# Half-size transposes on both row halves, a new order of a step, and padded last rows in a local-attention branch

## The chip, the cores and the metric

The kernel runs on one core of a Trainium2 chip. A core has a TensorE (PE, with its weight loads shown apart as PEld), a VectorE (DVE), a ScalarE (ACT), a GpSimd (POOL) and queues that issue DMAs (SyncE, SP, here). Each engine works through its own instructions in the order in which they were issued and waits on semaphores for the others. PE writes its results to PSUM, of which there are eight banks of 128 partitions by 512 fp32 values, and DVE or ACT carry them from there to SBUF. The metric is the time of one execution in microseconds (us) as the device takes it.

## The reference

The input `x` has 2 sequences of 2048 tokens with 256 features, all in fp32. It is normalized first (`xn`), and then

- the first branch `s` is a global attention with 16 heads of 16 features and a spatial bias on the first 257 rows and columns, a projection, and a layer norm of `xn` added to it;
- the second branch is two layers of a local transformer on `xn`, and `g` is the SiLU of what it returns;
- the output is `x + s * g`.

A layer of the second branch is, for every sequence:

```
h   = shift_token(x)                     # second half of the features comes from the token before
q,k,v = split(h @ wqkv)                  # 8 heads of 64
q,k = l2norm(q)*q_scale, l2norm(k)*k_scale, then rotary with the xpos scale
o   = softmax(mask(8 q k^T)) v           # windows of 128, each sees itself and the window before
x   = x + o @ wo
h   = layernorm(shift_token(x))*lg + lb
a,g = split(h @ w1 + b1)                 # 2 x 682
x   = x + (a * gelu(g)) @ w2 + b2
```

682 is five blocks of 128 and 42 rows more.

## The kernel before

`global_attention` computes the first branch and puts it into DRAM (`s_out`). It takes the first 1790 us and is not touched. `ffn_branch` computes the second branch and the output.

**Tiling.** The residual stream lies transposed in SBUF, features on partitions, as `xA[b]`, one tile for each sequence. The branch walks through 16 chunks (`slots`): layer, chunk of 512 tokens, sequence, in that order from the outermost. A chunk (`s`) has four tiles of 128 tokens (`i`), which are also the attention's windows. The loop at the end of the function takes one step for every tile, `n = 4 s + i`, and four more to drain. In a step several tiles are in work at once: `cur` is the tile of the step, `pre` the one before it and `pre2` the one before that.

**The pieces of a step.** The order of the instructions on each engine is the order in which the code issues them (the scheduler is off: `tc.manual_schedule()`). The string `STEP` gives the order of the pieces, and `FIRST_STEP` that of the first nine steps:

- `Q`, `K`, `V` (`a_project`, L844): the projection of `cur`, two products of 512 columns each. DVE multiplies Q and K out of PSUM by the rotary tables (L861 to L863), ACT squares them (L865) and POOL adds the two halves of the rotation (L866). `norm`, issued after the next piece but one, sums the squares (L870), takes a maximum with a tiny number (L874) on DVE, the power -1/2 (L875) and the product (L876) on POOL. V is copied by ACT (L850).
- `T0`, `T1` (`a_turn`, L888): four transposes of `pre`'s rotated Q and K by PE into one bank, and one copy to SBUF, of Q by ACT (L891) and of K by DVE (L894).
- `S0`, `S1` (`a_scores`, L913): the scores of `pre`, for four of the eight heads each. A head has 64 features, so that two heads, on rows 0 to 63 and 64 to 127 of the array, go into two banks. DVE adds the mask and takes the maximum (L926), ACT exponentiates with a running sum (L934), DVE inverts the sums (L940) and POOL multiplies by them (L948); in the first eight tiles ACT does this (L945).
- `W0`, `W1` (`a_weights`, L961): the transposes of the attention weights, eight of 128x128 for four heads, and their copies, by DVE for the first four heads (L968) and by ACT for the others (L966).
- `A0`, `A1` (`a_sums`, L982): weights times V, with the output on 64 partitions, and after `A1` a copy by ACT (L990).
- `F`: what else is due in this step for older chunks: the variance product `pv` (`f_var`, L1034) at `i = 0`, the attention's output projection `px` (`a_out`, L997) at `i = 1`, half of the second feed-forward product (`f_out`) at `i = 2` and at `i = 3`, the sum over the halves (`f_add`) at `i = 2` and the mean product `pm` (`f_mean`, L1020) at `i = 3`.
- `G`: so many of the 11 gate pieces of a chunk (`f_gate`, L1071, and `f_last`, L1092), five at `i = 0` of the next chunk and before that 2, 3 and 2 at `i` = 1, 2, 3. A gelu piece (ACT, L1076) and a product piece (DVE, L1080) alternate. The last piece takes the 42 last columns of both halves in one product (L1092), with its gelu at L1095 and its product at L1097.

In `STEP` the weights (`W`) and sums (`A`) are those of `pre`, in `FIRST_STEP` the small letters `w` and `a` mean those of `pre2`. The tenth step has an order of its own that does both.

**Small pieces between.** `soon(k, f)` issues `f` after `k + 1` more pieces. The layer norm's square root (ACT, L1037), its inverse in four reciprocals of 128 columns (DVE, L1044) and its two scalings (L1049, L1050) are spread over the pieces in this way from the end of `F` at `i = 0`. `gates` keeps what is to be issued at the end of the next `F`.

**The feed-forward output** (`f_out`). In layer 0 it is transposed, `py` (L1112), six products of 512 columns for 128 features, the last of them on 42 rows. In layer 1 tokens are on partitions, `pz` (L1131), six products of 256 columns for 128 tokens, the last again on 42 rows, and the residual is added in PSUM by two more products with the identity (L1136). DVE adds `b2` (L1141), ACT takes the SiLU (L1144), POOL multiplies by `s` and adds `x` (L1145, L1146), and a DMA writes it out.

**Banks.** All PE results of the branch take the eight PSUM banks in turn (`bank`), so that a product waits until the bank of the eighth one back has been read.

Of the kernel before, what the change touches and what calls it, by code (L numbers as in the profile page):

```python
# [11 lines left out]
F32 = mybir.dt.float32  # L12
# [6 lines left out]
P = 128  # L19
# [15 lines left out]
HID = 682  # L35
NM = (HID + P - 1) // P
MASKED = -1e30


@with_exitstack  # L40
# [624 lines left out]
def ffn_weights(tc, t, own, s_pool):  # L665
# [61 lines left out]
    def load_2(l):  # L727
        W["2"] = W["pool"].tile([P, NM, D], F32, tag="w2", name=f"w2_{l}")
        full = HID // P
        nc.sync.dma_start(  # L730
            W["2"][:, :full, :], t["w2"][l, : full * P, :].rearrange("(m p) n -> p m n", p=P)
        )
        nc.sync.dma_start(W["2"][: HID - full * P, full, :], t["w2"][l, full * P :, :])

    mask = own.tile([P, 2 * P], F32, name="mask")
# [17 lines left out]

STEP = "T0 T1 Q S0 S1 V K F G W0 W1 G A0 A1 G".split()

FIRST_STEP = "Q T0 w0 w1 T1 K a0 a1 S0 G S1 V F G G".split()
N_FIRST = 8


def ffn_branch(tc, t, xA, s_out, weights, ident, eps_t, mean_w, vecs, b2_row, x_ch, out_ch):
# [8 lines left out]
    with ExitStack() as ctx:  # L771
# [108 lines left out]
        def a_turn(s, i, n):  # L880

            l, b, cc = slots[s]
            ti = cc * TPC + i
            nm = f"{s}_{i}_{n}"
            rf = st[s, i]["rot"][n].rearrange("p h d -> p (h d)")
            ps = bank(f"pt_{nm}", (P, 4, P))
            for c in range(4):
                nc.tensor.transpose(ps[:, c, :], rf[:, c * P : (c + 1) * P], ident)  # L888
            x = pool.tile([P, 4, P], F32, tag="qT" if n == 0 else f"kT{b}", name=f"xT_{nm}")
            if n == 0:  # L890
                nc.scalar.copy(x, ps)  # L891
                st[s, i]["qT"] = x
            else:
                nc.vector.tensor_copy(x, ps)  # L894
                kvs[l, b, ti, "k"] = x

        def parts_of(s, i):
# [54 lines left out]
        def a_weights(s, i, hb):  # L952

            S = st[s, i]
            parts = parts_of(s, i)
            p0 = parts[0][0]
            for r in range(2):
                ps = bank(f"pw_{s}_{i}_{hb}_{r}", (P, 2, 2, P))
                for x in range(2):
                    for pa, _ in parts:  # L960
                        nc.tensor.transpose(  # L961
                            ps[:, x, pa, :], S["sm"][hb, r][:, x, pa * P : (pa + 1) * P], ident
                        )
                pT = pool.tile([P, 2, 2, P], F32, tag="pT", name=f"pT_{s}_{i}_{hb}_{r}", bufs=4)
                if hb == 1:
                    nc.scalar.copy(pT[:, :, p0:, :], ps[:, :, p0:, :])  # L966
                else:
                    nc.vector.tensor_copy(pT[:, :, p0:, :], ps[:, :, p0:, :])  # L968
                S["pT", hb, r] = pT

        def a_sums(s, i, hb):
            l, b, cc = slots[s]
            S = st[s, i]
            parts = parts_of(s, i)
            if hb == 0:
                S["po"] = bank(f"po_{s}_{i}", (P, 4, P))
            for x in range(2):
                c = 2 * hb + x
                for pa, kt in parts:
                    for r in range(2):  # L980
                        h = 2 * c + r
                        nc.tensor.matmul(  # L982
                            S["po"][r * HD2 : (r + 1) * HD2, c, :],
                            kvs[l, b, kt, "v"][:, h * HD2 : (h + 1) * HD2], S["pT", hb, r][:, x, pa, :],
                            start=(pa == parts[0][0]), stop=(pa == 1),
                        )
# [70 lines left out]
        def f_gate(s, m, n):  # L1057

            l, b, cc = slots[s]
            nm = f"{s}_{m}_{n}"  # L1060
            V = vecs[:, l, :]
            mw = min(P, HID - m * P)
            at = n * HID + m * P
            if mw < P:
                return f_last(s, m, mw)
            hc = fs[s]["hc"]
            if not fs[s].get("ready"):
                all_due()
            ps = bank(f"pg_{nm}")
            for k in range(2):  # L1070
                nc.tensor.matmul(  # L1071
                    ps[:mw], W["1"][:, k, at : at + mw], hc[:, k, :], start=(k == 0), stop=(k == 1)
                )
            if n == 1:
                gl = pool.tile([P, CH], F32, tag="gl", name=f"gl_{nm}")
                nc.scalar.activation(gl[:mw], ps[:mw], AF.Gelu, bias=V[:mw, NM + m : NM + m + 1])  # L1076
                fs[s]["gl"] = gl
            else:
                u = pool.tile([P, CH], F32, tag="u", name=f"u_{nm}", bufs=9)
                nc.vector.scalar_tensor_tensor(  # L1080
                    u[:mw], ps[:mw], V[:mw, m : m + 1], fs[s]["gl"][:mw], ALU.add, ALU.mult
                )
                fs[s]["u"].append(u)

        def f_last(s, m, mw):

            l = slots[s][0]
            V = vecs[:, l, :]
            hc = fs[s]["hc"]
            ps = bank(f"pg_{s}_{m}")  # L1090
            for k in range(2):
# [4 lines left out]
            u = pool.tile([P, CH], F32, tag="u", name=f"u_{s}_{m}", bufs=9)  # L1096
            nc.vector.scalar_tensor_tensor(  # L1097
                u[:mw], ps[:mw], V[:mw, m : m + 1], gl[:mw], ALU.add, ALU.mult
            )
            fs[s]["u"].append(u)  # L1100

        def f_out(s, k, part):

# [3 lines left out]
            if l < DEPTH - 1:  # L1107
                if part == 0:
                    F["py"] = bank(f"py_{s}_{k}")
                for m in range(3 * part, 3 * part + 3):  # L1110
                    mw = min(P, HID - m * P)
                    nc.tensor.matmul(  # L1112
                        F["py"], W["2"][:mw, m, k * P : (k + 1) * P], F["u"][m][:mw],
                        start=(m == 0), stop=(m == NM - 1),
                    )
                if part == 1:
# [2 lines left out]
                return  # L1119
            if part == 0:  # L1120
                F["py"] = bank(f"pz_{s}_{k}", (P, 2, D))
                F["s"] = pool.tile([P, 2, D], F32, tag="s", name=f"s_{s}_{k}")
                F["x"] = pool.tile([P, 2, D], F32, tag="x", name=f"x_{s}_{k}")
                F["y"] = pool.tile([P, 2, D], F32, tag="y", name=f"y_{s}_{k}")
# [2 lines left out]
            i = 2 * k + part  # L1127
            ps = F["py"][:, part, :]
            for m in range(NM):
                mw = min(P, HID - m * P)  # L1130
                nc.tensor.matmul(  # L1131
                    ps, F["u"][m][:mw, i * P : (i + 1) * P], W["2"][:mw, m, :], start=(m == 0), stop=False
                )
# [33 lines left out]
        for n in range(len(tiles) + 4):  # L1167
            s, i = divmod(n, TPC)
            cur, pre, pre2 = (tiles[x] if 0 <= x < len(tiles) else None for x in (n, n - 1, n - 2))
            order = FIRST_STEP if n <= N_FIRST else STEP  # L1170
            if n == N_FIRST + 1:
                order = "w0 w1 T0 T1 Q a0 a1 S0 S1 F V K G W0 W1 G A0 A1 G".split()

            def have(x):
                return 0 <= x < n_slots
# [15 lines left out]
            else:  # L1191
# [28 lines left out]
            for op in order:  # L1220
                j = int(op[1:] or 0)
                if op[0] in "QKV":
                    if cur:
                        piece(lambda: a_project(*cur, "QKV".index(op)))
                elif op[0] in "TSWA":
# [129 lines left out]
```

## Time and profile before

| | |
|---|---|
| median of 3 runs | 3244.5 us (3231.96 to 3244.63) |
| profiled execution | 3238.24 us |
| its span, first to last instruction | 3236.1 us |
| granted TensorE clock in it | 0.993 |
| second branch, first `pp` of L844 to the end | 1798.2 to 3236.1 us |
| PE busy from 1926 to 2500 us | 571.8 of 574 us |
| PE busy from 2500 to 3123 us | 623.0 of 623 us |
| DVE, ACT, POOL busy from 2500 to 3123 us | 386.1, 363.6, 377.6 us |

A line of the chain reads: start and length in us, engine, the tile that is written, the line of the code, and how many instructions are merged. An fp32 product is two instructions, a transpose is one. A line of the groups reads: line, engine, operation, tiles written and read, shapes (partitions x elements), number of instructions, busy time and mean duration in ns of one, and then the idle time of the engine just before them with what ended it. PE's products are pipelined, so one lasts longer (592 ns at 512 columns) than the distance from it to the next (430 ns).

### The profile page before, as it was taken

Reading aid. Unit: us, or ns where it says so; the run is one execution under the profiler, and the core shown is the slowest. Engines: PE = TensorE matmul, PEld = TensorE weight load, DVE = VectorE, ACT = ScalarE, POOL = GpSimd, SP = SyncE. Lnnn points to the kernel's source line nnn. Section 1 sums busy time; section 2 is a strip of 40 time slices with the busy share of each in tenths; the row PEclk is TensorE's granted clock in tenths of the full one; section 3 lists DMA queues with packets and bytes.
Section 4 is the critical chain, followed back from the end, with each engine's and each line's share of the span. In section 5 each row is a group of like instructions: output and inputs, shape, how many; then the busy total and the mean of one; then the engine's idle time right before and its main releaser. Section 6 shows DMA issues by size and latency. Waiting matters only on the chain.

```text
span 3236.1 us, 55622 instructions
## 1 busy us (share of the span) xinstructions
PE 3187.6 (99%) x20844; PEld 1584.3 (49%) x20844; DVE 2242.0 (69%) x4761; ACT 2059.6 (64%) x4220; POOL 1234.9 (38%) x1100
## 2 busy tenths in 40 slices
PE   8999999999999999999999899999999999999999
PEld 3444444444444444444443455555555556666665
DVE  6898888877777777777772566666666666666652
ACT  3677776677776777777777566555555555555652
POOL 3222223112221121221212655666555555665642
PEclk9999999999999999999999999999999999999999
DMA  3100101000001100000000100000000000000001
GB/s 113 28 8 19 36 11 31 24 9 20 20 26 47 43 20 12 12 25 5 7 15 19 67 9 1 8 1 7 1 27 7 1 19 26 17 14 20 21 20 52
DMA packets 65826, 70.34 MB, mean 22 GB/s; under 512 B 28745, under 2 KB 44189, under 8 KB 65557
## 3 DMA queue, kind: packets, MB, share of 16 engines
q1 hardware_dynamic: 64658, 66.00, 6.9%
q8 instruction: 165, 2.70, 0.3%
q14 instruction: 105, 0.85, 0.1%
q10 hardware_dynamic: 386, 0.52, 0.0%
q0 software_dynamic: 512, 0.26, 0.0%
HBM read 45.26 MB, written 17.53 MB: 19 GB/s over the span
## 4 chain that ended last, share of the span: by engine, by line
PE 91%; DVE 3%; issue 2%; ACT 2%; POOL 1%; DMA 1%; SPq 0%; POOLq 0%; DVEq 0%; ACTq 0%
PE pm L400 19%; PE ps L442 16%; PE po L461 15%; PE pp L844 9%; PE pg L1071 7%; PE po L982 3%; PE ps L913 3%; PE px L997 3%; PE pw L961 3%; PE py L1112 3%; PE pt L888 2%; PE pz L1131 2%; PE px L571 1%; ACT sm L934 1%; PE pp_wk L332 1%
## 5 line engine op out<-in xcount | busy, mean ns | idle before, releaser
L403 DVE TENSOR_REDUCE mx<-pm 128x1 f32<-128x512 f32 x2048 | 1260.3, 682 | 325.7 <-PE ps L442 304.0
L444 ACT ACTIVATE e<-ps 128x512 f32<-128x512 f32 x2048 | 1052.9, 604 | 192.7 <-PE ps L442 182.0
L400 PE MATMUL pm<-kT,qT 32*128 32x512 f32 x4096 | 1134.5, 620 | 0.1
L442 PE MATMUL ps<-qa,kT 32*128 32x512 f32 x4096 | 1095.8, 625 | 1.7 <-ACT e L444 1.7
L472 POOL TENSOR_TENSOR o<-o,part 128x512 f32<-128x512 f32 x224 | 284.0, 1268 | 1301.2 <-ACT part L471 1289.6
L400 PEld LDWEIGHTS pm<-kT,qT 32*128 32x128 f32 x4096 | 481.0, 184 | 358.3 <-DVE mx L403 241.4
L442 PEld LDWEIGHTS ps<-qa,kT 32*128 32x128 f32 x4096 | 441.7, 184 | 224.1 <-ACT e L444 180.7
L461 PE MATMUL po<-e,v 128*32 128x512 f32 x4096 | 495.9, 602 | 1.9 <-DVE mx L403 1.9
L844 PE MATMUL pp<-weights,xA 128*128 128x512 f32 x768 | 359.1, 604 | 0.8 <-DVE s L576 0.8
L866 POOL TENSOR_TENSOR rot<-rot,swp 128x512 f32<-128x512 f32 x128 | 166.5, 1302 | 397.5 <-DVE swp L863 397.2
L1071 PE MATMUL pg<-hc,weights 128*128 128x512 f32 x640 | 298.1, 596 | 0.0
L471 ACT COPY part<-po 128x512 f32<-128x512 f32 x224 | 131.2, 586 | 249.9 <-PE po L461 247.6
L461 PEld LDWEIGHTS po<-e,v 128*32 128x32 f32 x4096 | 108.1, 109 | 351.5 <-DVE mx L403 174.4
L934 ACT ACTIVATE sm<-sm,wmx 128x256 f32<-128x256 f32 (+1 forms) x512 | 249.5, 488 | 7.8 <-DVE wmx L926 7.0
L875 POOL TENSOR_TENSOR rn<-rn,mhalf 128x8 f32<-128x8 f32 x128 | 210.8, 1647 | 100.8 <-DVE rn L874 97.9
L865 ACT ACTIVATE sqq<-pp 128x512 f32<-128x512 f32 x128 | 76.3, 596 | 268.0 <-DVE swp L863 259.6
L948 POOL TENSOR_TENSOR sm<-sm,wls 128x512 f32<-128x512 f32 (+1 forms) x224 | 222.4, 1024 | 10.0 <-DVE wls L940 10.0
L844 PEld LDWEIGHTS pp<-weights,xA 128*128 128x128 f32 x768 | 136.5, 191 | 132.9 <-issue 123.6
L926 DVE CUSTOM_DVE_ANT_0 sm<-ps,mask 128x256 f32<-128x256 f32 (+1 forms) x512 | 180.6, 409 | 1.3 <-PE ps L913 1.0
L1071 PEld LDWEIGHTS pg<-hc,weights 128*128 128x128 f32 x640 | 115.0, 190 | 121.3 <-issue 116.2
L894 DVE COPY xT<-pt 128x512 f32<-128x512 f32 x64 | 43.2, 676 | 145.4 <-PE pt L888 145.4
L961 PE MATMUL pw<-ident,sm 128*128 128x128 f32 x992 | 130.5, 278 | 11.1 <-ACT sm L945 8.2
(164 smaller groups left out, 3425.1 us busy)
## 6 DMA issues: line engine op xcount, KB each, us to landing
s<-in_x_dram SPq DMA_DIRECT2D x8, 512.0 KB
qk_wk<-stage_wk SPq DMA_DIRECT2D x16, 256.0 KB
kT<-qk_wk SPq DMA_DIRECT2D x128, 32.0 KB
qk_wq<-stage_wq SPq DMA_DIRECT2D x16, 256.0 KB
qT<-qk_wq SPq DMA_DIRECT2D x128, 32.0 KB
qa<-qk_wq SPq DMA_DIRECT2D x128, 32.0 KB
s_out<-s SPq DMA_DIRECT2D x8, 512.0 KB
s<-s_out SPq DMA_DIRECT2D x16, 256.0 KB
```

The lines of the kernel that those rows point to most:

```text
L400: nc.tensor.matmul(ps, qT[rows, q0 : q0 + P], kT[rows, c * CH : (c + 1) * CH], start=True, stop=True)
L403: nc.vector.tensor_reduce(mxs[n][:, j * TPC + i, c : c + 1], ps, AX.X, ALU.max)
L442: nc.tensor.matmul(ps, kT[rows, kt * P : (kt + 1) * P], qas[n % 2][rows, :], start=True, stop=True)
L444: nc.scalar.activation(e, ps, AF.Exp)
L461: nc.tensor.matmul(pos[n][j * HP : (j + 1) * HP, :], v[:, kt, (r + j) * VW : (r + j) * VW + HP], es.pop((n, kt, j)), start=(kt % 2 == 0), ...
L472: nc.gpsimd.tensor_add(os[n], os[n], part)
L844: nc.tensor.matmul(ps, xA[b][:, k, at : at + P], W["qkv"][:, k, n * INNER : (n + 1) * INNER], start=(k == 0), stop=(k == 1),)
L875: nc.gpsimd.tensor_tensor(rn, rn, mhalf, ALU.pow)
L934: nc.scalar.activation(sm[:, x, lo:], sm[:, x, lo:], AF.Exp, scale=-1.0, bias=mx[:, hb, r, x : x + 1], accum_out=ls[:, hb, r, x : x + 1],)
L948: nc.gpsimd.tensor_mul(sm, sm, ls[:, hb, r, :, None].to_broadcast([P, 2, 2 * P - lo]))
L961: nc.tensor.transpose(ps[:, x, pa, :], S["sm"][hb, r][:, x, pa * P : (pa + 1) * P], ident)
L1071: nc.tensor.matmul(ps[:mw], W["1"][:, k, at : at + mw], hc[:, k, :], start=(k == 0), stop=(k == 1))
```

## The change

- **Transposes by halves.** `T` and `W` split each 128x128 transpose into two, on rows 0 to 63 and on rows 64 to 127, each with a 64x64 corner of the identity and 64 columns of output. The two halves write to two banks, so `T0` and `T1` take two banks each instead of one. A copy of `T` becomes two copies of 256 elements a partition. `W` had one bank and one copy for each pair of heads and has one for each row half now; the copies keep their size.
- **Order.** `STEP` begins with `T`, `W`, `S` and `A`, and `W` and `A` are always those of `pre2`. `Q`, `K`, `V`, `F` and three `G` follow. The tenth step loses its own order. The gate pieces are 5, 2, 2, 3.
- **The last 42 rows.** The product of the last gate goes to a tile of its own, `u_last`, whose other rows are zeroed once, and the other rows of the last block of `w2` are zeroed before its DMA, so that the last product of `py` and `pz` has 128 rows.
- **The last residual.** In layer 1 the residual is transposed into a bank of its own (`pzx`) instead of being added in PSUM; DVE adds `b2` to it and then the product.

```diff
+HALVES = [slice(r * HD2, (r + 1) * HD2) for r in range(2)]
...
+        nc.gpsimd.memset(W["2"][:, full, :], 0.0)
...
-STEP = "T0 T1 Q S0 S1 V K F G W0 W1 G A0 A1 G".split()
-
-FIRST_STEP = "Q T0 w0 w1 T1 K a0 a1 S0 G S1 V F G G".split()
+STEP = "T0 T1 W0 W1 S0 S1 A0 A1 Q K V F G G G".split()
+
+FIRST_STEP = "Q T0 W0 W1 T1 K A0 A1 S0 G S1 V F G G".split()
...
+        u_last = cp.tile([P, CH], F32, name="u_last")
+        nc.gpsimd.memset(u_last, 0.0)
...
-            ps = bank(f"pt_{nm}", (P, 4, P))
+            pss = [bank(f"pt_{nm}_{r}", (P, 4, HD2)) for r in range(2)]
             for c in range(4):
-                nc.tensor.transpose(ps[:, c, :], rf[:, c * P : (c + 1) * P], ident)
+                for r, rows in enumerate(HALVES):
+                    nc.tensor.transpose(pss[r][:, c, :], rf[rows, c * P : (c + 1) * P], ident[rows, rows])
             x = pool.tile([P, 4, P], F32, tag="qT" if n == 0 else f"kT{b}", name=f"xT_{nm}")
+            for r, rows in enumerate(HALVES):
+                (nc.scalar.copy if n == 0 else nc.vector.tensor_copy)(x[:, :, rows], pss[r])
...
-            for r in range(2):
-                ps = bank(f"pw_{s}_{i}_{hb}_{r}", (P, 2, 2, P))
-                for x in range(2):
+            pss = [bank(f"pw_{s}_{i}_{hb}_{q}", (P, 2, 2, 2, HD2)) for q in range(2)]
+            for x in range(2):
+                for r in range(2):
                     for pa, _ in parts:
-                        nc.tensor.transpose(
-                            ps[:, x, pa, :], S["sm"][hb, r][:, x, pa * P : (pa + 1) * P], ident
-                        )
...
+                        for q, rows in enumerate(HALVES):
+                            nc.tensor.transpose(
+                                pss[q][:, x, r, pa, :], S["sm"][hb, r][rows, x, pa * P : (pa + 1) * P],
+                                ident[rows, rows],
+                            )
+            pT = pool.tile([P, 2, 2, 2, P], F32, tag="pT", name=f"pT_{s}_{i}_{hb}")
+            for q, rows in enumerate(HALVES):
+                (nc.scalar.copy if hb == 1 else nc.vector.tensor_copy)(
+                    pT[:, :, :, p0:, rows].rearrange("p x r a q -> p (x r) a q"),
+                    pss[q][:, :, :, p0:, :].rearrange("p x r a q -> p (x r) a q"),
+                )
...
             nc.vector.scalar_tensor_tensor(
-                u[:mw], ps[:mw], V[:mw, m : m + 1], gl[:mw], ALU.add, ALU.mult
+                u_last[:mw], ps[:mw], V[:mw, m : m + 1], gl[:mw], ALU.add, ALU.mult
             )
...
                     nc.tensor.matmul(
-                        F["py"], W["2"][:mw, m, k * P : (k + 1) * P], F["u"][m][:mw],
+                        F["py"], W["2"][:, m, k * P : (k + 1) * P], F["u"][m],
...
-                nc.tensor.matmul(
-                    ps[:, h * P : (h + 1) * P], xA[b][:, h, at : at + P], ident, start=False, stop=(h == 1)
-                )
+                nc.tensor.transpose(F["xt"][:, part, h * P : (h + 1) * P], xA[b][:, h, at : at + P], ident)
             if part == 1:
-                nc.vector.tensor_add(y, F["py"], b2_row[:, None, :].to_broadcast([P, 2, D]))
+                nc.vector.tensor_add(y, F["xt"], b2_row[:, None, :].to_broadcast([P, 2, D]))
+                nc.vector.tensor_add(y, y, F["py"])
...
-            if n == N_FIRST + 1:
-                order = "w0 w1 T0 T1 Q a0 a1 S0 S1 F V K G W0 W1 G A0 A1 G".split()
...
-                ng = (5, 2, 3, 2)[i]
+                ng = (5, 2, 2, 3)[i]
...
-                        piece(lambda: {"T": a_turn, "S": a_scores, "W": a_weights, "A": a_sums}[op[0]](*pre, j))
-                elif op[0] in "wa":
+                        piece(lambda: (a_turn if op[0] == "T" else a_scores)(*pre, j))
+                elif op[0] in "WA":
                     if pre2:
-                        piece(lambda: {"w": a_weights, "a": a_sums}[op[0]](*pre2, j))
+                        piece(lambda: (a_weights if op[0] == "W" else a_sums)(*pre2, j))
```

More of the change, by code (lines that the diff above doesn't have):

```diff
@@ L885, in a_turn @@
             rf = st[s, i]["rot"][n].rearrange("p h d -> p (h d)")
-            ps = bank(f"pt_{nm}", (P, 4, P))
+            pss = [bank(f"pt_{nm}_{r}", (P, 4, HD2)) for r in range(2)]
             for c in range(4):
-                nc.tensor.transpose(ps[:, c, :], rf[:, c * P : (c + 1) * P], ident)
+                for r, rows in enumerate(HALVES):
+                    nc.tensor.transpose(pss[r][:, c, :], rf[rows, c * P : (c + 1) * P], ident[rows, rows])
             x = pool.tile([P, 4, P], F32, tag="qT" if n == 0 else f"kT{b}", name=f"xT_{nm}")
+            for r, rows in enumerate(HALVES):
+                (nc.scalar.copy if n == 0 else nc.vector.tensor_copy)(x[:, :, rows], pss[r])
             if n == 0:
-                nc.scalar.copy(x, ps)
                 st[s, i]["qT"] = x
             else:
-                nc.vector.tensor_copy(x, ps)
                 kvs[l, b, ti, "k"] = x
@@ L956, in a_weights @@
             p0 = parts[0][0]
-            for r in range(2):
-                ps = bank(f"pw_{s}_{i}_{hb}_{r}", (P, 2, 2, P))
-                for x in range(2):
+            pss = [bank(f"pw_{s}_{i}_{hb}_{q}", (P, 2, 2, 2, HD2)) for q in range(2)]
+            for x in range(2):
+                for r in range(2):
                     for pa, _ in parts:
-                        nc.tensor.transpose(
-                            ps[:, x, pa, :], S["sm"][hb, r][:, x, pa * P : (pa + 1) * P], ident
-                        )
[L964 to L969, printed above, removed]
+                        for q, rows in enumerate(HALVES):
[9 more added lines that the diff above has]
+                )
+            S["pT", hb] = pT
         def a_sums(s, i, hb):
@@ L983, in a_sums @@
                             S["po"][r * HD2 : (r + 1) * HD2, c, :],
-                            kvs[l, b, kt, "v"][:, h * HD2 : (h + 1) * HD2], S["pT", hb, r][:, x, pa, :],
+                            kvs[l, b, kt, "v"][:, h * HD2 : (h + 1) * HD2], S["pT", hb][:, x, r, pa, :],
                             start=(pa == parts[0][0]), stop=(pa == 1),
@@ L1078, in f_gate @@
             else:
-                u = pool.tile([P, CH], F32, tag="u", name=f"u_{nm}", bufs=9)
+                u = pool.tile([P, CH], F32, tag="u", name=f"u_{nm}", bufs=8)
                 nc.vector.scalar_tensor_tensor(
@@ L1095, in f_last @@
             nc.scalar.activation(gl[:mw], ps[h : h + mw], AF.Gelu, bias=last_b[h : h + mw, l : l + 1])
-            u = pool.tile([P, CH], F32, tag="u", name=f"u_{s}_{m}", bufs=9)
             nc.vector.scalar_tensor_tensor(
-                u[:mw], ps[:mw], V[:mw, m : m + 1], gl[:mw], ALU.add, ALU.mult
+                u_last[:mw], ps[:mw], V[:mw, m : m + 1], gl[:mw], ALU.add, ALU.mult
             )
-            fs[s]["u"].append(u)
+            fs[s]["u"].append(u_last)
         def f_out(s, k, part):
@@ L1110, in f_out @@
                 for m in range(3 * part, 3 * part + 3):
-                    mw = min(P, HID - m * P)
                     nc.tensor.matmul(
-                        F["py"], W["2"][:mw, m, k * P : (k + 1) * P], F["u"][m][:mw],
+                        F["py"], W["2"][:, m, k * P : (k + 1) * P], F["u"][m],
                         start=(m == 0), stop=(m == NM - 1),
@@ L1121, in f_out @@
                 F["py"] = bank(f"pz_{s}_{k}", (P, 2, D))
+                F["xt"] = bank(f"pzx_{s}_{k}", (P, 2, D))
                 F["s"] = pool.tile([P, 2, D], F32, tag="s", name=f"s_{s}_{k}")
@@ L1129, in f_out @@
             for m in range(NM):
-                mw = min(P, HID - m * P)
                 nc.tensor.matmul(
-                    ps, F["u"][m][:mw, i * P : (i + 1) * P], W["2"][:mw, m, :], start=(m == 0), stop=False
+                    ps, F["u"][m][:, i * P : (i + 1) * P], W["2"][:, m, :], start=(m == 0),
+                    stop=(m == NM - 1),
                 )
@@ L1224, in ffn_branch @@
                         piece(lambda: a_project(*cur, "QKV".index(op)))
-                elif op[0] in "TSWA":
+                elif op[0] in "TS":
                     if pre:
-                        piece(lambda: {"T": a_turn, "S": a_scores, "W": a_weights, "A": a_sums}[op[0]](*pre, j))
-                elif op[0] in "wa":
+                        piece(lambda: (a_turn if op[0] == "T" else a_scores)(*pre, j))
+                elif op[0] in "WA":
                     if pre2:
-                        piece(lambda: {"w": a_weights, "a": a_sums}[op[0]](*pre2, j))
+                        piece(lambda: (a_weights if op[0] == "W" else a_sums)(*pre2, j))
                 elif op == "F":
```

## The prediction

> **What bounds the kernel now.** I read the page first, then the waits and the groups of the second branch (1790 us to the end), then the chain of waits in stretches of one to four steps, then the timelines of VectorE (DVE), ScalarE (ACT) and GpSimd (POOL) across one step boundary.
>
> The page, engine shares and the engines of the chain that ended last:
> ```profile
> PE 3187.6 (99%) x20844; PEld 1584.3 (49%) x20844; DVE 2242.0 (69%) x4761; ACT 2059.6 (64%) x4220; POOL 1234.9 (38%) x1100
> ...
> PE 91%; DVE 3%; issue 2%; ACT 2%; POOL 1%; DMA 1%; SPq 0%; POOLq 0%; DVEq 0%; ACTq 0%
> ```
> The chain of waits from 2380 to 2480 us (start, length, what):
> ```profile
> 2408.74 5.34 PE py L1112 x12
> 2414.08 1.05 PE pm L1020 x2
> ...
> 2422.22 1.02 PE pt L888 x8
> 2423.24 1.72 PE pp L844 x4
> 2424.96 1.99 PE ps L913 x32
> 2426.95 3.63 PE pp L844 x8
> 2430.57 0.86 PE pv L1034 x2
> 2431.43 3.43 PE pg L1071 x8
> 2434.87 1.75 PE pw L961 x16
> ...
> 2440.05 1.90 PE po L982 x32
> 2441.95 1.02 PE pt L888 x8
> ```
> From one `pt` to the next is one step (one query tile), here 19.73 us, and in it TensorE (PE) goes from piece to piece without a hole. So in the steady part of the branch PE work taken away shortens the step, until another engine is late. An ordinary product of 512 columns is two instructions of 0.43 us (3.43 for eight); a 128x128 transpose is one of 0.109 (1.75 for sixteen). The scores `ps`, 64 rows each, go two at a time: 32 instructions in 1.99 us. Pieces beside another shape of array are longer: `pp` x8 takes 3.63 after `ps` where `pg` x8 takes 3.43, and `pt` x8 takes 1.02 after `po` where half of `pw` is 0.875. So a switch costs 0.15 to 0.20 us.
>
> Weight loads of the second branch, by group:
> ```profile
> L913 PEld LDWEIGHTS ps<-xT,xT 64*128 64x128 f32 x1984 | 115.8, 188 | 44.5 <-issue 43.6 <-ACT xT L891 0.5 <-DVE xT L894 0.2
> ...
> L961 PEld LDWEIGHTS pw<-ident,sm 128*128 128x128 f32 x992 | 111.7, 141 | 54.4 <-issue 27.7 <-ACT sm L945 19.0 <-POOL sm L948 6.7
> L982 PEld LDWEIGHTS po<-pT,v 128*64 128x64 f32 x1984 | 108.2, 137 | 49.3 <-issue 26.5 <-ACT pT L966 11.0 <-DVE pT L968 10.2
> ```
> The DVE timeline around the step boundary at 2441.95:
> ```profile
> 2440.86 0.74 DVE L1097 SCALAR_TENSOR_TENSOR u<-pg,vecs,gl 42x512 f32<-42x512 f32 x1
> 2441.52 1.75 DVE L1044 RECIPROCAL rs<-rs 128x128 f32<-128x128 f32 x2
> 2443.20 0.62 DVE L894 COPY xT<-pt 128x512 f32<-128x512 f32 x1
> ```
> The reader should see that the keys' copy sits in DVE's queue behind the last gate's product and two reciprocals and ends 1.9 us after `pt` began. Today nobody minds: `pt` and a projection (1.02 + 1.72) come before the scores.
>
> **The change part by part.**
>
> *Half-size transposes.* 1504 transposes (992 `pw`, 512 `pt`) become as many pairs, one half on rows 0 to 63 and one on rows 64 to 127, each moving 64 columns and loading 128. The trace has no such pair, so I bound its interval. From below: half the columns of 0.109, so 0.055 us. From above, if the halves do share the array: the pair of scores, which loads 128 columns into 64 rows and takes (1.99 - 0.20)/16 = 0.112; then nothing is gained. Between them the loads decide. Ordinary loads last 188 ns for 128 columns and 137 for 64, 0.8 ns a column, so some 85 ns are fixed; a transpose's load of 128 columns lasts only 141, so about 56 ns move data. I take 0.06 us a pair, near the lower end, because that row is a transpose itself. Gain on PE: 1504 x 0.049 = 74 us.
>
> The Trainium skill ("TensorE: Matmul & The Clock Gate", section "LDWEIGHTS (loading the stationary operand)") speaks against this: a load takes its columns over 1.2 ns whatever the rows, an estimate of 107 ns for these halves. By it the pair stays at 0.107 and this term is 3 us, by the 141 ns row it is 74; the measured transpose load contradicts the rule, so I go by the row.
>
> *The new order.* A step becomes T, W, S, A, Q, K, V, F, G, with W and A of two tiles back. The weights' transposes no longer wait for the softmax of their own step. But between T and S stands only W: with the halves S could start after 24 x 0.06 + 0.19 for the switch = 1.63 us, where 2.74 us lay between before. It needs the copies of both transposes. Each copy becomes two of 256 elements: on DVE 0.335 + 0.415 us (256-element rows last 0.415, overlapping by 0.08), on ACT at most 2 x 0.49 (the 256-element exponential; 0.45 taken). In front of them, by step of the chunk:
> - Step 0: ACT still has the gelu of the last gate product (PE delivers 0.16 us after T starts; gelu 0.69): 0.89, then the query copies to 1.8; S at 1.85, 0.2 late.
> - Step 1: the last piece before T is now the 42-row gate (before, `po` of 1.90 us came after it). Gelu to 0.89, its product on DVE to 1.67, a reciprocal (0.93) to 2.5, the key copies to 3.2; S at 3.25, 1.6 late.
> - Steps 2 and 3: a gate product (0.74) to 0.93, key copies to 1.62; S at 1.65: nothing.
>
> So 1.85 us a chunk; the new order runs in 14 of 16 chunks: 26 us back. Were there no wait it would be 0; were ACT and DVE each another 1 us behind at every boundary, 14 x 4 = 56 more.
>
> Behind S, in step 0: the masks (8 x 0.345) end at 5.7, ACT's table load (1.28) and eight exponentials (0.49 each) at 8.2, and DVE's second reciprocal, which waits for them, at 8.5. The products of Q and K now queue behind it on DVE (before, Q's came ahead of the masks): 9.9 and 11.1. POOL: four normalizing products of 1.0 from 6.5 to 10.6, two sums of 1.27 to 13.2, then twice a power of 1.65 and a product of 1.04: K's rotated tile is ready at 18.7. The next T needs K about 0.25 after it starts, at 18.9 in this shortest step (19.73 - 1.18 gained - 0.1 switch + 0.2 wait, plus 0.25). A margin of 0.2 is thinner than my errors, so I charge 0.5 us in the 14 steps of this kind, 7 us; ends 0 and 2 us there and 1 in step 2, 42 us. Step 1, with two more reciprocals ahead of the masks and the scaling behind them, comes to 21.7 against 22.7.
>
> *Switches.* In the new order the array changes shape three times a step instead of four (in to T, S to A, A to Q): 0.1 us x 55. The first nine steps have K between W and A and change five times instead of three: 9 x 0.38. Net -2 us, ends -8 and +4.
>
> *42 rows padded.* 48 products on 42 rows (16 `py`, 32 `pz`) lose both switches: `py` x12 takes 5.34 where twelve are 5.15, and the two `pm` after it 1.05 instead of 0.86. 48 x 0.38 = -18 us. The zeroing of `W["2"]` on POOL lies whole steps ahead of its readers (0.3 us by the 128x256 memset row of `weights`). `u_last` is one buffer, but is rewritten after the four output pieces that read it have gone by.
>
> *Residual by transposes.* The 64 identity products of two instructions (four take 0.64 us with the switch, 0.44 without) become transposes of one: 32 x 0.22 = -7 us. DVE gets 16 more sums of 0.61 us, which only the last exposes: +0.4. The gates' 2, 2, 3 in place of 2, 3, 2 move 1.72 us between steps. At the end a tile's A stands right before `px`, which then waits some 0.8 us for the copy: +1 with the sum.
>
> Sum: -74 + 26 + 7 - 2 - 18 - 7 + 1 = -67 us. The profiled execution took 3238.2 us (span 3236.1); the median shown is 3244.5 over a spread of 12.7, so I put the forecast 2 us above 3171: **3173 us**.
>
> **Rivals.**
> 1. *No new wait, all PE time saved:* copies keep up. 74 + 2 + 18 + 7 - 1 = 100 us, so 3138. For it: DVE is 69% and ACT 64% busy. Against: the boundary above.
> 2. *Loads bound the halves* (0.109 to 0.112 a pair, as `ps` shows): nothing from the transposes, and S then starts at 2.75, so only step 1's wait (0.5) stays: about -20, so 3218.
> 3. *The rotated keys come late* on POOL in steps 0 and 2: 35 us beyond the forecast, 3208; a full 1 us in every step brings it to about 3235.
> 4. *Slower: the halves take turns.* If two transposes on different row halves don't overlap, a pair costs 0.218, so 1504 x 0.109 = +164 against -26 from the rest: about 3375. It turns slower once a pair exceeds 0.109 + 26/1504 = 0.126. For it: no row here shows transposes side by side. Against: `ps` runs in pairs with both loads and products overlapped.
>
> **How the numbers follow.** Forecast 0.45 (its own range 3145 to 3205), rival 1 0.13, rival 2 0.15, rival 3 0.15, rival 4 0.10, and 0.02 unnamed. A measurement of this kernel can tell about 0.5%, 16 us, from no change. Faster: the forecast, rival 1, most of 2 and two thirds of 3: 0.78; same: 0.09; slower: rival 4 and the end of 3, 0.13. The range 3130 to 3235 leaves out rival 4, the tails below rival 1 and beyond rival 3.
>
> **What would show it.** In the profile after: intervals of `pt` and `pw` halves near 0.06 us a pair (0.11 is rival 2, 0.22 rival 4); idle PE ahead of `ps`, released by the key copy on DVE and the query copy on ACT, most of it in step 1; idle ahead of `pt` released by POOL's `rot` (rival 3); `py` x12 at 5.15. I would be wrong above all if a third engine's queue, not PE, sets the step length throughout.

## The result, and the profile after

The changed kernel takes **3194.4 us** (median of 4 runs, 3189.9 to 3197.2) against 3244.2 (3232.0 to 3244.6) for the kernel before: a ratio of **0.985**, 95% interval 0.983 to 0.988. The forecast was 3173 in a range of 3130 to 3235. The profiled execution took 3196.3 us (span 3194.6, granted clock 0.989), so the two profiled executions differ by 41.9 us, where the sum gave 67.

The page of the changed kernel, engine shares and the engines of the chain that ended last:

```profile
PE 3111.0 (97%) x22284; PEld 1542.8 (48%) x22284; DVE 2243.4 (70%) x4841; ACT 2059.5 (64%) x4284; POOL 1244.8 (39%) x1103
...
PE 81%; DVE 7%; ACT 5%; POOL 3%; issue 3%; DMA 0%; POOLq 0%; SPq 0%; ACTq 0%; DVEq 0%
```

PE has 1440 instructions more and 77 us less to do, and its share of the chain fell from 91% to 81%: there are places now where PE waits. The chain of waits of the changed kernel, from 2340 to 2440 us (start, length, what), shows one such place and then the steps that run as meant:

```profile
2344.89 0.36 PE pg L1101
...
2346.70 0.69 ACT gl L1104
...
2347.41 0.74 DVE u_last L1105
2348.16 0.86 DVE rs L1053
2349.02 0.60 DVE xT L897 x2
2349.62 0.86 DVE rs L1053
2350.48 1.14 DVE pT L974 x2
2351.62 0.86 DVE rs L1053
...
2352.84 1.28 ACT L940
...
2354.13 4.05 ACT sm L940 x16
...
2358.39 1.25 DVE hc L1058
...
2359.66 1.15 DVE hc L1059
...
2369.21 1.05 POOL rot L881
...
2370.31 0.46 PE pt L894 x8
2370.77 1.00 PE pw L968 x32
2371.77 1.84 PE ps L919 x32
...
2389.44 0.65 PE pt L894 x16
2390.09 1.00 PE pw L968 x32
2391.08 1.84 PE ps L919 x32
...
2400.17 5.15 PE py L1119 x12
2405.32 0.86 PE pm L1029 x2
```

From the last gate (2344.89) to `pt` of step 2 (2370.31), 25 us, the chain does not touch PE: it goes from the gelu through DVE's reciprocals, the masks, ACT's table load and exponentials, the two scalings of `hc` and the rotation to POOL. PE has other work for most of that time: it stands idle for 1.5 us of it, 0.8 us ahead of `pw`, `ps` and `po` in step 1 and 0.6 us ahead of `pt` of step 2. In the two steps that follow PE goes from piece to piece, and `py` and `pm` take 5.15 and 0.86 in it, where they took 5.34 and 1.05.

The span by stretches, from the starts of the output projections `px` (16 instructions each) in the PE timelines of both kernels:

| stretch | before, us | after, us | difference |
|---|---|---|---|
| first branch (same code) | 1798.2 | 1792.2 | -6.0 |
| its end to `px` of the third chunk | 218.9 | 233.9 | +15.0 |
| to `px` of the eighth, five chunks of layer 0 | 432.2 | 417.5 | -14.7 |
| to `px` of the ninth | 84.0 | 81.9 | -2.1 |
| to `px` of the sixteenth, seven chunks of layer 1 | 607.6 | 578.6 | -29.0 |
| to the end | 95.3 | 90.5 | -4.8 |

The chunks gained 2.9 us each in layer 0 and 4.1 in layer 1. The surprise is the second row: the first three chunks became 15 us longer. The first row says how far such a table can be trusted: the same code took 1792 to 1803 us from run to run in the profiles of this study.

### The profile page after: what moved, and what is told of

Same layout as the page of the kernel before. It is cut to its first block, busy times and chain, and to the rows that moved or that the text cites. A ratio compares the mean times of both kernels' runs of the same rounds, so it can differ in the third digit from the quotient of the medians.

```text
span 3194.6 us, 58744 instructions
## 1 busy us (share of the span) xinstructions
PE 3111.0 (97%) x22284; PEld 1542.8 (48%) x22284; DVE 2243.4 (70%) x4841; ACT 2059.5 (64%) x4284; POOL 1244.8 (39%) x1103
## 4 chain that ended last, share of the span: by engine, by line
PE 81%; DVE 7%; ACT 5%; POOL 3%; issue 3%; DMA 0%; POOLq 0%; SPq 0%; ACTq 0%; DVEq 0%
PE pm L401 20%; PE ps L443 16%; PE po L462 15%; PE pp L849 8%; PE pg L1080 5%; PE po L991 3%; PE py L1119 3%; PE ps L919 3%; ACT sm L940 2%; PE pz L1138 2%; POOL rn L880 1%; PE pw L968 1%; PE px L572 1%; PE pp_wk L333 1%; DVE rs L1053 1%
## 5 line engine op out<-in xcount | busy, mean ns | idle before, releaser
L954 POOL TENSOR_TENSOR sm<-sm,wls 128x512 f32<-128x512 f32 (+1 forms) x224 | 236.8, 1088 | 405.8 <-DVE wls L946 405.8
L1080 PE MATMUL pg<-hc,weights 128*128 128x512 f32 x640 | 284.3, 592 | 0.0
L849 PEld LDWEIGHTS pp<-weights,xA 128*128 128x128 f32 x768 | 143.6, 195 | 167.1 <-issue 162.6
L1089 DVE SCALAR_TENSOR_TENSOR u<-pg,vecs,gl 128x512 f32<-128x512 f32 x80 | 60.1, 751 | 151.2 <-ACT gl L1085 82.3
L919 PE MATMUL ps<-xT,xT 64*128 64x128 f32 x1984 | 132.9, 282 | 6.9 <-DVE xT L897 6.9
```

Source lines behind the costliest of these rows:

```text
L849: nc.tensor.matmul(ps, xA[b][:, k, at : at + P], W["qkv"][:, k, n * INNER : (n + 1) * INNER], start=(k == 0), stop=(k == 1),)
L919: nc.tensor.matmul(pss[r][:, x, pa * P : (pa + 1) * P], S["qT"][rows, 2 * hb + x, :], kvs[l, b, kt, "k"][rows, 2 * hb + x, :], start=True, ...
L954: nc.gpsimd.tensor_mul(sm, sm, ls[:, hb, r, :, None].to_broadcast([P, 2, 2 * P - lo]))
L1080: nc.tensor.matmul(ps[:mw], W["1"][:, k, at : at + mw], hc[:, k, :], start=(k == 0), stop=(k == 1))
```

## The experiments

The theory, once the result was in: the parts that take work from PE give what was summed where PE sets the pace; a chain of the other engines takes part of it back at the boundary after step 1; and in the first nine steps, where ACT also does the normalizing, PE is not what limits. The rivals were that the halves give less than 0.049 us each, that the new order by itself loses far more, and that the early loss is only noise or is the granted clock's doing. "Before" below is always the kernel before on the same chip. No experiment leaves out a part of the computation.

### One part at a time

**Padding and the residual alone**, on the kernel before:

```diff
+        nc.gpsimd.memset(W["2"][:, full, :], 0.0)
...
-                        F["py"], W["2"][:mw, m, k * P : (k + 1) * P], F["u"][m][:mw],
+                        F["py"], W["2"][:, m, k * P : (k + 1) * P], F["u"][m],
...
-                    ps[:, h * P : (h + 1) * P], xA[b][:, h, at : at + P], ident, start=False, stop=(h == 1)
+                nc.tensor.transpose(F["xt"][:, part, h * P : (h + 1) * P], xA[b][:, h, at : at + P], ident)
```

> The kernel before with only the 42 rows padded and the last residual by transposes. My theory: 48 products lose both switches (18 us) and 32 pairs of identity products become transposes (7 us), nothing else changes: 3219 us, and py x12 takes 5.15 us. Rival 'a switch is hidden anyway': 3240 or more.

Measured: 3214.0 us (3213.8 to 3215.9) against 3243.2, a ratio of 0.992 (0.990 to 0.993), so 29 us where the sum had 25. The chain of waits of this kernel:

```profile
2408.22 5.15 PE py L1113 x12
2413.37 0.86 PE pm L1023 x2
```

These are the lengths of an unbroken run of products. Six products of which the last has 42 rows cost two changes of the array's shape, and giving that last one 86 rows of zeros costs nothing on PE.

**The order with full transposes**, which is the changed kernel with `T` and `W` as they were:

```diff
-                for r, rows in enumerate(HALVES):
-                    nc.tensor.transpose(pss[r][:, c, :], rf[rows, c * P : (c + 1) * P], ident[rows, rows])
+                nc.tensor.transpose(ps[:, c, :], rf[:, c * P : (c + 1) * P], ident)
...
-                            nc.tensor.transpose(
-                                pss[q][:, x, r, pa, :], S["sm"][hb, r][rows, x, pa * P : (pa + 1) * P],
-                                ident[rows, rows],
-                            )
+                        nc.tensor.transpose(
+                            ps[:, x, pa, :], S["sm"][hb, r][:, x, pa * P : (pa + 1) * P], ident
+                        )
```

> The changed kernel with full 128x128 transposes in T and W again (one bank and one copy each, as before); its order, the padding and the residual by transposes stay. My theory: the halves take 74 us of TensorE work away but their copies and reciprocals give much of it back as waits ahead of S and T in step 1 of a chunk, and the first nine steps lose some 8 us more because the clock drops there; so here T and W take 2.62 us again, the wait in step 1 shrinks from 1.6 to 0.4 us, the clock stays up: 3222 us, some 28 above the changed kernel. Rival 'the halves are worth all their work': 3268. Rival 'the halves are worth nothing': 3194.

Measured: 3226.0 us (3223.7 to 3227.7) against 3243.2, 0.995 (0.994 to 0.996). It has padding and residual too, so the order alone costs 12 us (3226 against 3214). The halves on top of it are then worth 32 us (3226 to 3194), not 74. So the halves fall short by far more than the order loses.

**The halves alone in the old order:**

```diff
-                nc.tensor.transpose(ps[:, c, :], rf[:, c * P : (c + 1) * P], ident)
+                for r, rows in enumerate(HALVES):
+                    nc.tensor.transpose(pss[r][:, c, :], rf[rows, c * P : (c + 1) * P], ident[rows, rows])
```

(and `W` in the same way as in the change).

> The kernel before with only the half-size transposes, in the old order of a step. My theory: 74 us of work less, but T and W now stand alone between products on 128 rows, so four more switches of 0.19 us in 55 steps (42 us) and some 8 us by the clock in the first nine steps: 3220 us, with no wait ahead of S. Rival 'the halves are worth nothing': 3286. Rival 'a switch costs nothing': 3178.

Measured: 3228.9 us (3224.8 to 3232.0) against 3243.2, 0.996 (0.995 to 0.997). The old order puts each `pw` between two gate pieces, and the chain of waits shows what a pair of 64-row transposes does to its neighbours:

```profile
2424.14 1.72 PE pg L1076 x4
2425.85 1.14 PE pw L964 x32
2426.99 1.91 PE pg L1076 x4
```

`pw` takes 1.14 instead of 1.00 us and the gate behind it 1.91 instead of 1.72, so of the 0.75 us that halving saves (1.75 to 1.00), two changes of shape take back 0.33. The row-tiled pieces have to stand together, as the new order has them: there they follow each other at 0.65, 1.00, 1.84. So the new order spares the halves these changes of shape, and its price is the waits below. In the totals the two nearly cancel: halves in the old order (14 us less) and padding (29 us less) would add up to some 3200 us, an estimate, against 3194 for the changed kernel. What the new order can give shows only when its waits are taken out, as in the next section.

### The boundary after step 1

The reciprocals stand in DVE's queue between the copies that the scores wait for, and the masks stand behind them. Issuing them earlier, by one, two, three and five pieces, takes them out from between the copies:

```diff
-                    soon(2 * q + 1, lambda q=q: invert(q))
+                    soon((0, 1, 2, 2)[q], lambda q=q: invert(q))
```

> The changed kernel with the four reciprocals of the layer norm issued after the first three gate pieces of step 0, ahead of the last gate's product, instead of spread over T and W of step 1. My theory: in step 1 VectorE is free after the last gate's product at 1.67 us, S starts at 2.4 instead of 3.2 us after T, the masks and so K's chain end 2.6 us earlier, and step 2 loses its wait of 0.75: 1.6 us in 14 chunks, 3172 us. Rival 'the gelu of the last gate on ScalarE alone sets step 1': 3194, S still 3.2 late.

Measured: 3181.7 us (3178.4 to 3188.7) against 3243.2, 0.981 (0.980 to 0.983), 13 us below the changed kernel. The chain of waits of this kernel at the same boundary:

```profile
2350.23 0.36 PE pg L1101
...
2351.43 1.67 DVE rs L1053 x2
2353.10 0.57 DVE u_last L1105
...
2353.71 0.71 PE pw L968 x15
2354.42 1.84 PE ps L919 x32
```

The stretch off PE is 3 us long instead of 25. The chunks went from 83.5 to 81.6 us in layer 0 and from 82.7 to 81.6 in layer 1; that is 17 us over the twelve. What is left is a wait of `pw` for the product of the last gate: it needs the bank which that product reads, and two of the reciprocals still stand ahead of that product on DVE.

The rest goes if the projection V comes last in a step, between the gates and the transposes, so that the last gate's product is out of the way before `T` and `W` need its bank. The key's normalization is issued one piece earlier and the scalings a little later to suit, and the reciprocals stay early:

```diff
-STEP = "T0 T1 W0 W1 S0 S1 A0 A1 Q K V F G G G".split()
+STEP = "T0 T1 W0 W1 S0 S1 A0 A1 Q K F G G G V".split()
...
-            soon(1, norm)
+            soon(1 - n if s * TPC + i > N_FIRST else 1, norm)
...
-                soon(2 * TPC + 2, lambda: scale(0))
-                soon(2 * TPC + 3, lambda: scale(1))
+                soon(2 * TPC + 3, lambda: scale(0))
+                soon(2 * TPC + 4, lambda: scale(1))
```

> The changed kernel with the early reciprocals and with V moved from after K to the end of the step, so that V's product of 1.72 us stands between the last gate product and T (K's norm is issued one piece earlier so that it stays ahead of F). My theory: the last gate's gelu and product are done before T, the copies start at once, S starts 1.6 us after T in every step and no bank is waited for: 0.7 us in step 1 and some 0.2 to 0.5 in the others against the early reciprocals alone, 3171 us. Rival 'K's chain on GpSimd sets the steps': the time stays at 3182, and idle time ahead of T by the rotated keys takes the place of that ahead of S.

Measured: 3176.5 us (3174.8 to 3179.6) against 3241.6, 0.980 (0.979 to 0.982). The PE waits of the changed kernel between 2100 and 2440 us are these (what waited, for what, us in all, times, longest):

```profile
PE ps L919 <- DVE xT L897: 2.7, 5, 0.8
PE pt L894 <- POOL rot L881: 2.5, 4, 0.6
PE po L991 <- DVE pT L974: 1.4, 5, 0.7
PE pw L968 <- DVE u_last L1105: 0.8, 4, 0.2
```

With the reciprocals early, only one row is left,

```profile
PE pw L968 <- DVE u_last L1105: 1.8, 5, 0.4
```

and with V last there is none. Chunks take 81.0 us in layer 0 and 80.7 in layer 1.

### The first nine steps

**Full transposes in the first nine tiles only**, halves from then on:

```diff
+            if s * TPC + i <= N_FIRST:
+                ps = bank(f"pt_{nm}", (P, 4, P))
+                for c in range(4):
+                    nc.tensor.transpose(ps[:, c, :], rf[:, c * P : (c + 1) * P], ident)
+                copy(x, ps)
+            else:
```

(and `W` in the same way).

> The changed kernel with full 128x128 transposes for the first nine tiles alone. In those steps TensorE waits for ScalarE's softmax, and the shorter transposes leave it idle enough that its granted clock falls to 0.5 in stretches of 3.4 or 6.8 us (time lost at half clock in the branch 27 us by the trace, 5 before). Theory 'clock': the stretches at half clock mostly go, the way to the third chunk's output projection is some 9 us shorter: 3185 us. Rival 'copies': the early steps are slow because the copies of T and W come late, two halves at once; then the stretches stay or cost nothing, 3194 us.

Measured: 3188.4 us (3186.5 to 3191.6) against 3241.6, 0.984 (0.983 to 0.985). So more work for PE, and 6 us less than the changed kernel; the two sets of runs just overlap (3189.9 to 3197.2 there), so by the totals alone the gain is not shown.

**Each half transposed twice** in the first nine tiles, which is twice the work of PE for the same result:

```diff
+                for again in range(2 if s * TPC + i <= N_FIRST else 1):
                     for r, rows in enumerate(HALVES):
```

(and `W` in the same way).

> The changed kernel with every half-size transpose of the first nine tiles issued twice, to the same place, so that TensorE has about as much to do there as with full transposes and everything else (banks, copies, order) is as in the changed kernel. Theory 'clock': more work keeps the clock up and the kernel gets faster, 3188 us, with fewer stretches at half clock. Rival 'copies': the extra transposes (some 200 pairs of 0.06 us) cost time or hide in the wait, 3194 to 3206 us.

Measured: 3195.4 us (3182.7 to 3201.7) against 3241.6, 0.985 (0.983 to 0.987). This could not be told from the changed kernel, so both ran again side by side:

> The changed kernel as it is, beside the next one on the same chip, because the two before were timed in different rounds: 3194 us, some 27 us lost at half clock in the branch.

Measured (the changed kernel again): 3193.2 us (3189.9 to 3202.5) against 3244.0, 0.986 (0.984 to 0.989).

> The changed kernel with each half-size transpose of the first nine tiles issued twice, again, beside the changed kernel itself. Theory 'clock': the first three chunks take 7 us less, as the trace of the first time had it, and the whole kernel 3 to 8 us less than the changed kernel. Rival 'copies': not faster.

Measured (each half twice again): 3190.9 us (3186.7 to 3202.2) against 3244.0, 0.986 (0.983 to 0.988). The totals do not separate the two. The stretch itself does say something. One row from the windows of each kernel, from the first projection to `px` of the third chunk: stretch, its length, busy time and instructions of PE, PEld, DVE, ACT and POOL, the granted clock, DMA share, GB/s. Before:

```profile
1798.20:2017.10 218.90, 204.13 (x1269) 120.16 (x1270) 138.97 (x428) 137.60 (x367) 135.07 (x108) 0.98 0.08 26
```

The changed kernel, its first profile and its second:

```profile
1792.20:2026.20 234.00, 207.19 (x1549) 122.58 (x1550) 140.21 (x447) 141.84 (x394) 136.63 (x110) 0.90 0.07 25
```

```profile
1792.50:2021.00 228.50, 202.04 (x1548) 118.57 (x1549) 140.09 (x447) 141.57 (x394) 136.52 (x110) 0.93 0.08 25
```

Full transposes in the first nine tiles, then each half twice (its second profile had 226.1 us, PE busy for 204.6, clock 0.95), then the new order with full transposes throughout, from the first set of experiments:

```profile
1798.40:2021.10 222.70, 203.38 (x1348) 120.01 (x1349) 138.66 (x438) 140.87 (x385) 136.82 (x110) 0.96 0.08 26
```

```profile
1802.40:2029.60 227.20, 205.62 (x1948) 128.21 (x1949) 139.97 (x447) 141.55 (x394) 136.55 (x110) 0.96 0.08 25
```

```profile
1795.40:2020.40 225.00, 206.53 (x1268) 123.47 (x1269) 139.07 (x434) 140.90 (x381) 136.56 (x110) 0.96 0.08 25
```

The last row separates the order from the halves: without the halves the new order makes the stretch 4 to 6 us longer (against 221.0 with the padding alone and 218.9 before), and the halves add 9 us to that (3.5 in the second profile). The profiles of all thirteen runs fall into two groups. In the five that issue single halves in the first nine tiles (the changed kernel twice, the halves in the old order, the early reciprocals, V last) the stretch lasts 228.5 to 234.5 us at a mean clock of 0.90 to 0.93. In the eight with full or doubled transposes there it lasts 218.8 to 227.6 us at 0.94 to 0.98. So the loss is not noise, and it comes with the halves.

Length less PE's busy time is what PE stood idle: 14.8 us before, 26.8 and 26.5 in the changed kernel, 19.3 with full transposes, 21.6 and 21.5 with each half twice. Doubling adds 400 instructions, some 12.5 us at 0.0625 us a pair, and the stretch does not get longer (227.2 and 226.1 against 234.0 and 228.5). So in this stretch twice the transposes cost nothing. That does not prove that PE's work is without effect there, since the doubled kernels were also at half clock for less time, 18 and 20 us against 49 and 34. The PE waits of that stretch name what PE waits for; in the changed kernel:

```profile
PE pw L968 <- ACT sm L951: 10.8, 23, 0.9
PE pt L894 <- POOL rot L881: 9.7, 5, 2.2
PE pw L968 <- ACT rs L1046: 2.9, 1, 2.9
```

and before:

```profile
PE pw L961 <- ACT sm L945: 8.2, 13, 2.2
PE pt L888 <- POOL rot L876: 4.2, 2, 2.4
```

`pw` waits for ACT's normalizing and `pt` for POOL's rotation in both kernels; where PE comes sooner, it waits longer. All PE waits of the stretch add up to 15.3 us before and 27.2 after.

### Together

**Full transposes in the first nine tiles, early reciprocals and V last** (the edits of the three sections above):

> Both together: full transposes in the first nine tiles, early reciprocals, V last. If the first nine steps and the later steps are independent, the gains add: 3162 us. If K's chain on GpSimd is the bound in the later steps, about 3173.

Measured: 3169.6 us (3161.6 to 3175.7) against 3241.6, 0.978 (0.976 to 0.980). That is 7 us below V last without the full transposes, about the 6 us that these gave to the changed kernel, so the gains add; the 3162 expected took both larger than they were.

**The same with an order of its own for the tenth step**, where `pw` still waited for the softmax of the last tile of the old order (the earlier normalization of K begins one tile later, too):

```diff
+            if n == N_FIRST + 1:
+                order = "Q K V T0 T1 W0 W1 S0 S1 A0 A1 F G G G".split()
```

> The kernel with full transposes in the first nine tiles, early reciprocals and V last, and the tenth step alone in the order Q K V T W S A F G, because its weights belong to a tile whose softmax was issued late in the ninth step: TensorE waits some 4 us there for the softmax now, and some 13 us more in the three steps that follow, part of it at half clock. If that wait is what starts the rest: 3160 us. If it only moves: 3169.

Measured: **3163.5 us** (3162.7 to 3172.8) against 3244.0, **0.977** (0.975 to 0.979). It is the fastest kernel of the study, 31 us below the changed one; against the version without the tenth step's order the ranges of the runs overlap, and its first three chunks are no shorter (227.6 us against 226.9), so that last edit is not shown to help. A step of its chain of waits, which is PE alone (the left-out pieces are `px` and two gates, without a gap too):

```profile
2658.08 0.79 PE pt L902 x16
2658.87 1.00 PE pw L989 x32
2659.87 1.84 PE ps L926 x32
2661.71 1.90 PE po L1012 x32
2663.61 3.63 PE pp L849 x8
...
2677.78 1.72 PE pp L849 x4
2679.50 0.64 PE pt L902 x16
```

## Why the prediction came out as it did

The direction and the range were right; the forecast was 21 us too low. By its own steps:

- **"I take 0.06 us a pair"**: right. `pw` x32 takes 1.00 us in the chain, 16 pairs at 0.0625, and `pt` x16 0.65 with the switch. The loads, from the groups of the changed kernel:

```profile
L968 PEld LDWEIGHTS pw<-ident,sm 64*128 64x128 f32 x1984 | 75.1, 143 | 26.4 <-ACT sm L951 14.6 <-DVE u_last L1105 4.2 <-ACT rs L1046 3.1
```

  A load lasts 143 ns, as the 128x128 one did (141), but a pair of them and of transposes follows the next every 62.5 ns, so their records overlap. Rivals 2 (0.11 a pair) and 4 (0.22) fall. The reason is less sure than the size: the prediction had 0.055 from the 64 columns moved and 0.056 from the load, and no run separates the two. The Trainium skill ("TensorE: Matmul & The Clock Gate", section "LDWEIGHTS (loading the stationary operand)"), weighed in the prediction, divides the columns by 1.2, an estimate of 107 ns for these loads, and the prediction took from it a pair of 0.107 us. The measured load is 143 ns and the measured pair 0.0625 us, so the rule was no guide to either.
- **"Gain on PE: 1504 x 0.049 = 74 us"**: this is the step that failed. The price was right, the count was not. It took every transpose at the price of a stage in which PE has no holes, which had been read from the chain at 2380 to 2480 us and from a busy share of 571.8 of 574 us after 1926. In the first three chunks PE was idle for 14.8 of 218.9 us before the change, and the chain of waits there (1800 to 1960 us; the view ends the line early) has ACT's exponentials and normalizing as its two largest lines, while PE's lines add up to 29%:

```profile
by line: ACT sm L934 17.1%; ACT sm L945 11.8%; PE pp L844 11.1%; PE px L997 8.7%; DVE ss L870 6.0%; ACT sqq L865 4.6%; DVE rot L861 4.0%; DVE pT L968 3.8%; PE po L982 3.6%; PE pw L961 3.3%; POOL rn L875 3.1%; PE pt L888 2.4%; DVE rn L874 2.
```

  280 of the pairs lie there, 13.7 us of the 74; with the waits (2.4) and the switches of the first nine steps (3.4) the sum had that stretch 8 us shorter. It was 15.0 longer (9.6 in the second profile). That is 23 us (18) beside the 25 by which the sum missed the profiled execution, and the halves are 22 (17) of them: 13.7 expected that did not come, and the 9 (3.5) by which the stretch is longer than with full transposes in the same order. The steady chunks, the change of layer and the end account for another 8, and the first branch, 6 us shorter in that execution by chance, hid 6.
- **Waits ahead of S**: "Step 1 ... S at 3.25, 1.6 late". Measured 3.22 us from `pt` (2429.71 in the PE timeline) to `ps` (0.76 + 2.46), 1.7 beyond the 1.55 of the undisturbed steps. The size was right. The other steps were undisturbed.
- **"Step 0 ... K's rotated tile is ready at 18.7"**, charged at 0.5 us: this wait did not come; the step ends after 18.45 us and `pt` starts at once.
- **"Step 1, with two more reciprocals ahead of the masks and the scaling behind them, comes to 21.7 against 22.7"**: wrong. The tile was ready 23.7 us after `pt` (2346.54 to 2370.27), and step 2 waited, with PE idle for 0.6 us. The prediction gives no working for the 21.7, so which of its terms was 2 us short stays open. The chain shown above has what stands in the 23.7, and the ACT timeline of the changed kernel adds how the table load comes into it:

```profile
2352.84 1.28 ACT L940 ACT_TABLE_LOAD   x1 [2.80 <-DVE wmx L932]
```

  ACT stood idle for 2.80 us and began the load only when the first mask was done, so its 1.28 us stood on the chain; the two scalings (1.25 + 1.15) stood on it too, between the exponentials and the rotation. So rival 3's mechanism was there, one step later than I had put it. The charge for step 0 that was not needed happened, by luck, to cover most of it: the chunks' gains, 2.9 and 4.1 us, are 0.6 and 1.0 short of the 3.5 and 5.15 that the terms of the prediction (96 pairs, padding, switches and, in layer 1, the residual, less the two waits) give for a chunk of either layer. Moving the reciprocals, which are the nearest cause, gave back 17 us over twelve chunks.
- **42 rows and the residual**, -25: measured -29 alone. Its profile has 0.8 us a chunk in layer 0, where the terms give 0.76, and 2.0 in layer 1, where they give 2.4.
- **Rival 1**, no wait, 3138: it takes the whole order to get there. The fastest kernel's chunks are 5.5 us (layer 0) and 6.25 (layer 1) below those before; the terms of rival 1 make 5.9 and 7.5.

## What to carry to other kernels

Multiply a saving on an engine by the instructions of the stages in which that engine has no holes, and by no others: the stage in which PE already waited gave nothing back here, and even became longer. Pieces that use half of the array's rows belong next to each other, because each change of shape cost 0.14 to 0.19 us here, but bringing them together also brings together the copies that they wait for, and what else stands in those queues has then to be moved away from them. A late chain is best read from the piece that waits back to the first place where the engine that should lead is not on it; here that pointed at four reciprocals of 0.86 us that could run anywhere else.

## What was not expected of the hardware

In the first three chunks the granted clock of PE falls when PE's work gets less. In slices of 1.7 us over the first 102 us of the second branch, it is 1.00 or 0.50 and mixed only in the slices where it turns. It is at 0.50 for 6.8 us in all before the change, in one piece; for 32 us in the first profile of the changed kernel, in pieces of mostly 6.8; and for some 14 us in its second profile, in pieces of 3.4. Over the whole stretch it is at 0.50 for 10, 49 and 34 us, a mean of 0.98, 0.90 and 0.93, and 0.96 and 0.95 with each half transposed twice. The two profiles of the changed kernel differ by 5.5 us there, of which 5.2 is busy time of PE: the same products at another clock.

The Trainium skill ("TensorE: Matmul & The Clock Gate", section "A second HAM failure mode: psum-queue depth-cycling") says that many short idle times between groups of matmuls can make the clock go back and forth between half and full, and the pieces of 3.4 and 6.8 us at 0.50 agree with it. Another section of that page ("Part 4: PE-mode transpose") says that transposes do not count as busy in the same way as other products for the clock; the kernels with each transpose issued twice suggest that they do count, since their clock was higher in both profiles. What part of the early loss is clock and what part is waiting stays open: PE's idle time grew by 12 us in both profiles of the changed kernel, which is shown, but a slower clock also lengthens PE's own pieces in the chain through the other engines, and the totals with each half twice do not separate from those without. An estimate can be had from the two profiles of the changed kernel: 15 us more at half clock go with 5.4 us of length. At that rate the 39 and 24 us more at half clock than before the change would be 14 and 9 us, nearly all of the 15.0 and 9.6 by which the stretch is longer. The gain of 13.7 us that did not come would then be the waits' part. This rests on one pair of profiles and is not shown.
